# Scan products of two states by transposes on TensorE, 128-row products in the row norm and the last layer

## Chip, core and metric

The kernel runs on one core of a Trainium2 chip. The metric is the device time of one execution in microseconds (us). Three runs of the kernel before took 34249.87 to 34259.34 us, with a median of 34252.28. The engines are TensorE (PE, with its weight loads PEld), VectorE (DVE), ScalarE (ACT) and GpSimd (POOL). SyncE (SP) issues the DMAs of this stage. Each engine works through its own queue in the order of the program.

## The reference

Four layers follow each other on an image of 256 x 256 positions with 128 channels, each as x = x + layer(group norm of x). Layer 0 is an attention along rows, with a layer norm ahead of it (the "row norm"). Layer 1 is a selective scan in four directions. Layer 2 is a spectral layer with two small dense layers behind it. Layer 3 (the "last layer") is a gated recurrence of 16 steps with spectra of small kernels. Almost all of the change lies in the scan of layer 1:

```
x_dbl = einsum('bkdl,kcd->bkcl', xs, x_proj_w)
dts, Bs, Cs = split(x_dbl, [8, 8 + 16], axis=2)
delta = softplus(einsum(dts, dt_w) + dt_bias)
dA = exp(delta * A[d, n])
h[n] = dA * h[n] + (delta * x) * B[n]      # n = 0..15, one step for each position
y = sum over n of h[n] * C[n]
```

There are 256 inner channels d (two halves of 128, dh = 0 and 1), 16 states n, 65536 positions, and four directions k (rows, columns, and both backwards).

## The kernel before

The scan is done by `scan_stream`. A chunk is 512 positions of one direction, so there are 4 x 128 = 512 chunks, one after the other. Partitions are the 128 channels of one half, the free axis is positions. A chunk has eight steps s = 0..7, numbered through as g = 8 ch + s. Step s handles the half dh = s % 2 and the four states from 4 (s // 2) on. So steps 6 and 7 hold states 12 to 15. The loop is software-pipelined by hand: all engines run in program order, and the order of the lines in the loop is the order in each queue. The names used from here on:

- **b(j)**, the B product of step j, in the loop's count (b(8) to b(10) are steps 0 to 2 of the next chunk): delta * x times B for four states, 128 x 2048 elements, L763. GpSimd does steps 2, 4 and 6, VectorE the others. `b_order` says at which step a product is issued. The factor delta * x of the first half is in a PSUM bank (`mm`) with a copy in SBUF for GpSimd (L752); that of the second half is in the PSUM bank `du1`.
- **The scans**: each step has two, s6h0 and s6h1 for step 6. One scan, L796, runs over two states at once (1024 elements). Before it ScalarE writes exp(delta * A) for both states into one of two PSUM tiles `das` (L781, two activations), and then puts the carried state into the middle element of the B product (L785). Lists of extra work, `extras`, are issued behind each scan.
- **c(s)**, the C product, 128 x 2048, by GpSimd, L811.
- **sums(s)**: TensorE adds the four states of c(s) into the y bank with an identity matrix, L830, two steps later. Each product of 512 columns in float32 stands in the trace as two instructions.
- **For the next chunk**, in between: dt (L699, TensorE) and softplus on ScalarE (L711, L712, L718, L719) with a sum on TensorE (L725), delta * x on VectorE (L741), xproj (L667, TensorE), which gives B and C of the chunk after it; they go through DRAM.
- **The loads**: B and C come back from DRAM, spread over all partitions, as loads of 1 MB for four states each (L687 for B, L693 for C). A B load serves two products, b(2i) and b(2i + 1). B and C each have three buffers. At the end of the odd steps SP is given one B load and then one C load:

```python
if s % 2 == 1:
    load_b(g // 2 + 4)
    load_c(g // 2 + 3)
```

So the C load of s1 takes the buffer that c(0) and c(1) read. The results y are stored from step 2 of every even chunk (L643), 1 MB for two chunks, on the same queue.

In the row norm (`row_norm`, blocks of 2048 positions), TensorE centers (L141), takes variances (L163), and spreads the reciprocal root of each position over the partitions by a product with one row of ones (L183). In the last layer (64 blocks), products of 14 rows make the spectra (L1447), and VectorE does most of the gated steps; L1463 adds a constant and L1560 takes 1 - t, both on VectorE.

Of the kernel before, what the change touches and what calls it, by code (L numbers as in the profile page):

```python
# [10 lines left out]
F32 = mybir.dt.float32  # L11
# [16 lines left out]
class Ctx:  # L28


    def __init__(self, tc, t, pool):
        self.tc, self.nc, self.t = tc, tc.nc, t
        nc = self.nc
        self.ident = load(nc, pool, t["c_ident"], "ident")
        self.avg128 = load(nc, pool, t["c_avg128"], "avg128")
        self.gavg = load(nc, pool, t["c_gavg"], "gavg")
        self.ones = pool.tile([P, P], F32, name="ones")
        nc.vector.memset(self.ones, 1.0)
        self.eps = pool.tile([P, 1], F32, name="eps")
        nc.vector.memset(self.eps, 1e-5)  # L40

        self.stats = [pool.tile([P, NCH, 6], F32, name=f"stats{i}") for i in range(2)]
        self.pool = pool

# [6 lines left out]

def group_norm_coef(c, stats, name):

    nc = c.nc
    ab = c.pool.tile([P, 2], F32, name=f"ab_{name}")
    with c.tc.tile_pool(name=f"gn_{name}", bufs=1) as sb, c.tc.tile_pool(
        name=f"gnp_{name}", bufs=1, space=PSUM
    ) as ps:
        mv = sb.tile([P, 2], F32, name="gn_mv")
        nc.vector.bn_aggr(mv, stats)  # L60
        mean = ps.tile([P, 1], F32, name="gn_mean")
        nc.tensor.matmul(mean, c.gavg, mv[:, 0:1], start=True, stop=True)
        off = sb.tile([P, 1], F32, name="gn_off")
        nc.vector.tensor_tensor(off, mv[:, 0:1], mean, ALU.subtract)
        part = sb.tile([P, 1], F32, name="gn_part")
        nc.vector.scalar_tensor_tensor(part, off, off, mv[:, 1:2], ALU.mult, ALU.add)
        var = ps.tile([P, 1], F32, name="gn_var")
        nc.tensor.matmul(var, c.gavg, part, start=True, stop=True)
        sd = sb.tile([P, 1], F32, name="gn_sd")
        nc.scalar.activation(sd, var, AF.Sqrt, bias=c.eps)  # L70
        nc.vector.reciprocal(ab[:, 0:1], sd)
        nc.vector.scalar_tensor_tensor(ab[:, 1:2], mean, -1.0, ab[:, 0:1], ALU.mult, ALU.mult)
    return ab


# [26 lines left out]
def row_norm(c, x, zs, bs, ab):  # L102
# [6 lines left out]
    with ExitStack() as a:  # L109
# [14 lines left out]
        shift = one.tile([P, 1], F32, name="l0_shift")  # L124
        nc.vector.tensor_copy(shift, sp)
        scaled = one.tile([P, P], F32, name="l0_scaled")
        nc.vector.tensor_scalar(scaled, cent, ab[:, 0:1], None, ALU.mult)
# [51 lines left out]
        def spread(m):  # L179
            bc = bcs[m] = ps1.tile([P, 2, CH], F32, name="l0a_bc")  # L180
            for j in range(2):
                r = slice(32 * (m % 2 * 2 + j), 32 * (m % 2 * 2 + j) + 1)
                nc.tensor.matmul(bc[:, j], c.ones[r], rss[m // 2][r], start=True, stop=True)  # L183

# [387 lines left out]
def scan_stream(c, xc2, y, w):  # L572
# [5 lines left out]


    tc, nc = c.tc, c.nc  # L580
    G, BL, NG = 4, 1024, 8
    R = y[1].shape[3]
    NW = BL // S
    on_pool = (2, 4, 6)
    b_order = {0: (3,), 1: (4,), 2: (5,), 3: (6, 7), 4: (8,), 6: (10,)}
    chunks = []
# [4 lines left out]
    with ExitStack() as a:  # L591
# [7 lines left out]

        xds = [st.tile([64, CH], F32, name=f"l1b_xd{i}") for i in range(3)]  # L600
        for s in states:
# [5 lines left out]


        mm = ps1.tile([P, CH], F32, name="l1b_mm")
        du1 = ps1.tile([P, CH], F32, name="l1b_du")  # L610
        blocks, bcs, bbs, ccs, soft, dls, dbs, hs, hcs = ({} for _ in range(9))

# [62 lines left out]
        def xd_copy(ch):  # L675
            if ch >= N:
                return
            xd = xds[ch % 3]
            nc.scalar.copy(xd[:40], du1[:40])
            bc = bcs[ch] = dram.tile([32, CH], F32, name="l1b_bc")  # L680
            nc.sync.dma_start(bc, xd[8:40])

        def load_b(m):
            if m < 4 * N:
                n0 = m % 4 * G
                bb = bbs[m] = bcp.tile([P, G, CH], F32, name="l1b_bb")
                nc.sync.dma_start(bb, bcs[m // 4][n0 : n0 + G][None].to_broadcast([P, G, CH]))  # L687

# [7 lines left out]
        def dt(ch, dh):  # L696
            if ch >= N:
# [3 lines left out]
                w["dt"][:, chunks[ch][0], dh * P : dh * P + P],  # L701
                xds[ch % 3][0:41],
                start=True,
# [50 lines left out]
        def b_product(g):  # L754
            ch, j = divmod(g, NG)
            if ch >= N:
                return
            db = dbs[g] = wk.tile([P, G, CH], F32, name="l1b_db", bufs=5)
            if j in on_pool:
                eng, du = nc.gpsimd, dls[ch, "du"]  # L760
            else:
                eng, du = nc.vector, du1 if j % 2 else mm
            eng.tensor_tensor(db, bbs[g // 2], du[:, None, :].to_broadcast([P, G, CH]), ALU.mult)  # L763

        def scans(g, extras):
# [7 lines left out]
            for i in range(2):  # L773
                one, two = n0 + 2 * i + rev, n0 + 2 * i + 1 - rev
                da = das[i].rearrange("p g t -> p (g t)")
                if g == 0 or ch == N // 2 and j == 0:
                    nc.vector.memset(da[:, mid : mid + 1], 0.0)
                for n in (one, two):
                    o = n % 2 * CH
# [3 lines left out]
                    )  # L783
                first = db[:, 2 * i * CH + mid : 2 * i * CH + mid + 1]
                nc.scalar.activation(  # L785
                    first,
                    states[k][:, dh, two : two + 1],
                    AF.Identity,
                    scale=af[:, two : two + 1],
                    bias=first,  # L790
                )
                sl = slice(2 * i * CH, 2 * i * CH + 2 * CH)
                h_, a_, d_ = hf[:, sl], da, db[:, sl]
                if rev:
                    h_, a_, d_ = h_[:, ::-1], a_[:, ::-1], d_[:, ::-1]
                nc.vector.tensor_tensor_scan(  # L796
                    h_, a_, d_, states[k][:, dh, one : one + 1], ALU.mult, ALU.add
                )
                if i == 0 and g:
                    keep_state(g - 1)  # L800
# [49 lines left out]
        for m in range(3):  # L850
            load_b(m)
            load_c(m)
        for dh in range(2):
            dt(0, dh)
# [8 lines left out]
        b_product(2)  # L863
        load_b(3)
        for ch in range(N):
            nxt = ch + 1
            for s in range(NG):
# [7 lines left out]
                for j in b_order.get(s, ()):  # L875
                    b_product(NG * ch + j)
                extras = [[], []]
                if s == 1:
                    extras[1] = [lambda: soft_abs(nxt), lambda: y_out(ch - 1, 0)]
# [6 lines left out]
                if s == 5:  # L886
                    extras = [[lambda: soft_abs(nxt)], [lambda: soft_exp(nxt)]]
                if s == 6:
                    extras[1] = [lambda: xd_copy(ch + 2)]
                if s == 7:  # L890
                    extras[0] = [lambda: delta_x(nxt, 1), lambda: b_product(g + 2)]
                    extras[1] = [lambda: delta_copy(nxt, 1)]
                if s == 0:
                    dt(nxt, 0)
                scans(g, extras)
                if s == 2:
                    soft_sum(nxt)
                if s == 4:
                    dt(nxt, 1)
                if s == 5:  # L900
# [3 lines left out]
                if g >= 2:  # L904
                    sums(g - 2)
                c_product(g)
                if s % 2 == 1:
                    load_b(g // 2 + 4)
                    load_c(g // 2 + 3)
# [208 lines left out]

def layer1(c, x1, x2p, x2, ab, stats):
    tc = c.tc  # L1120
    with ExitStack() as ctx:
# [6 lines left out]
        with tc.tile_pool(name="l1_w", bufs=1) as wp:  # L1128
# [4 lines left out]
            scan_stream(c, (xc, xct), y, w)  # L1133
        scan_end(c, x1, ab, y[2], y[3], x2p, x2, stats)

# [244 lines left out]
def layer3(c, x3, out, spec, ab):  # L1380
# [9 lines left out]
    with ExitStack() as a:  # L1390
# [22 lines left out]
        nc.vector.tensor_scalar(less, c.ident, -1.0, None, ALU.mult)  # L1413
        phase = load(nc, one, t["c_phase_w"], "l3_phase")
        tiny = one.tile([P, 1], F32, name="l3_tiny")
# [19 lines left out]
        def spectra(b):  # L1435
# [3 lines left out]
            nc.sync.dma_start(k["x"], x3[:, bass.ts(b, BL)])  # L1439
            tu = io.tile([14, 4, 256], F32, name="l3_tu", bufs=2)  # L1440
            nc.sync.dma_start(tu, spec[bass.ts(b, 4)].rearrange("u r f -> r u f"))

# [19 lines left out]
            more = tmp.tile(half, F32, name="l3_more")  # L1462
            nc.vector.tensor_scalar(more, mag, 1e-8, None, ALU.add)  # L1463
            k["inv"] = inverse(more, 1.0, "l3_m")
# [49 lines left out]
        def steps(b):  # L1514
# [44 lines left out]
            have["x"] = new("x")  # L1559
            nc.vector.tensor_scalar(w["x"], w["t"], -1.0, 1.0, ALU.mult, ALU.add)  # L1560
            have["den"] = new("den")
# [72 lines left out]
def program(tc, t, out):  # L1634
    with ExitStack() as ctx:
# [7 lines left out]
        spec = dram.tile([S, 14, 256], F32, name="l3_spec")  # L1643
        with ExitStack() as a:
            kernel_spectra(c, spec, a)
            stream_stats(c, t["x"], c.stats[0])
        layer0(c, t["x"], x1, group_norm_coef(c, c.stats[0], "0"), c.stats[1])
        layer1(c, x1, x2p, x2, group_norm_coef(c, c.stats[1], "1"), c.stats[0])
        layer2(c, x2p, x2, x3, group_norm_coef(c, c.stats[0], "2"), c.stats[1])
        layer3(c, x3, out, spec, group_norm_coef(c, c.stats[1], "3"))  # L1650

# [90 lines left out]
```

## Time and profile before

| | us |
|---|---|
| median of three runs | 34252.28 |
| the profiled execution | 34251.71 |
| its span | 34249.9 |
| stretch from 8000 to 24000 us: scans | 5126 |
| VectorE's scans L796 in it, mean of one | 2.336 |
| GpSimd's C products L811 in it, mean of one | 4.528 |
| B products of VectorE L763, mean of one | 2.274 |
| TensorE instruction of a sum L830, mean of one | 0.639 |

The page gives busy time for each engine, then the span in 40 slices with a digit for the busy tenths, and the granted TensorE clock. A group of instructions reads: line, engine, operation, tiles written and read, shape, count, busy time, mean of one, and the idle time of the engine ahead of it with what ended it. On the timeline a row is: start, length, engine, line, operation, tiles, count, and in brackets the wait. Lengths of two instructions on one engine overlap a little at their ends, so the distance from start to start is what counts in a sum.

### The profile page before, as it was taken

How to read it: one execution, taken by the hardware profiler on the slowest of the kernel's cores; microseconds unless marked ns; L12 is line 12 of the kernel's file. 1: busy time of each engine (PE TensorE's matmuls, PEld its weight loads, DVE VectorE, ACT ScalarE, POOL GpSimd, SP SyncE). 2: the span in 40 equal slices, each digit the busy share in tenths (PEclk: the TensorE clock that was granted, in tenths of full speed). 3: DMA queues.
4: the chain of work that ended last, by engine and by line, in shares of the span. 5: the costliest groups of instructions: out<-in, count | busy, mean ns of one | idle time of the engine just before them, and what ended most of it. 6: DMA issues, size and time to landing. Idle time of an engine off the chain costs nothing. (4 is left out here: it accounts for less than half of the span.)

```text
span 34249.9 us, 256893 instructions
## 1 busy us (share of the span) xinstructions
PE 29062.3 (85%) x72308; PEld 12164.1 (36%) x72308; DVE 31137.1 (91%) x23801; ACT 22770.2 (66%) x46991; POOL 27433.4 (80%) x6996
## 2 busy tenths in 40 slices
PE   7999888888888888888888888888888888899988
PEld 3554333333333333333333333333333333334444
DVE  6668999999999999999999999999999999863699
ACT  3667777777777777777777777777777777532476
POOL 2446899999999999999999999999999999620000
PEclk8999999999999999999999999999999999999888
DMA  3113455555555555555555555555555555674111
GB/s 142 45 45 121 183 191 190 192 189 192 191 190 191 190 192 189 192 191 190 197 201 200 201 203 201 201 201 200 200 201 203 201 201 201 212 236 148 63 34 33
DMA packets 2076530, 5947.88 MB, mean 174 GB/s; under 512 B 115207, under 2 KB 1379608, under 8 KB 1499222
## 3 DMA queue, kind: packets, MB, share of 16 engines
q1 hardware_dynamic: 1939122, 5860.18, 47.3%
q10 hardware_dynamic: 135972, 71.27, 0.7%
q8 instruction: 570, 9.34, 0.1%
q14 instruction: 866, 7.09, 0.1%
HBM read 5238.41 MB, written 692.58 MB: 173 GB/s over the span
## 5 line engine op out<-in xcount | busy, mean ns | idle before, releaser
L796 DVE TENSOR_TENSOR_SCAN l1b_h<-l1b_da,l1b_state,l1b_db 128x1024 f32<-128x1024 f32 x8192 | 18792.7, 2336 | 596.9 <-ACT l1b_db L785 583.3
L811 POOL TENSOR_TENSOR l1b_hc<-l1b_h,l1b_cc 128x2048 f32<-128x2048 f32 x4096 | 18447.2, 4528 | 329.0 <-DVE l1b_h L796 328.0
L830 PE MATMUL l1b_y<-l1b_hc,ident 128*128 128x512 f32 x32768 | 16062.5, 639 | 1117.0 <-POOL l1b_hc L811 1117.0
L781 ACT ACTIVATE l1b_da<-l1b_dl,l_alog 128x512 f32<-128x512 f32 (+1 forms) x16384 | 11297.5, 690 | 3156.6 <-DVE l1b_h L796 2848.7
L830 PEld LDWEIGHTS l1b_y<-l1b_hc,ident 128*128 128x128 f32 x32768 | 6528.7, 205 | 10690.6 <-issue 8162.7
L763 POOL TENSOR_TENSOR l1b_db<-l1b_bb,l1b_dus 128x2048 f32<-128x2048 f32 x1536 | 6967.3, 4536 | 44.5 <-DMA l1b_bb<-l1b_bc 44.5
L763 DVE TENSOR_TENSOR l1b_db<-l1b_bb,l1b_du 128x2048 f32<-128x2048 f32 x2048 | 4657.8, 2274 | 35.2
L785 ACT ACTIVATE l1b_db<-l1b_state,l1b_db,l1b_af 128x1 f32<-128x1 f32 x8192 | 3045.2, 372 | 0.0
L699 PE MATMUL l1b_mm<-l1b_xd,l_dtw 41*128 41x512 f32 x2048 | 1373.1, 755 | 1712.6 <-ACT l1b_dus L752 1706.8
L725 PE MATMUL l1b_mm<-l1b_tail,ident 128*128 128x512 f32 x2048 | 1292.2, 717 | 1380.9 <-ACT l1b_tail L719 1378.5
L807 ACT COPY l1b_state<-l1b_h 128x4 f32<-128x4 f32 x4095 | 789.6, 193 | 2433.8 <-DVE l1b_h L796 2433.7
L327 POOL TENSOR_TENSOR l0b_e<-l0b_e,l0b_den 128x1024 f32<-128x1024 f32 x512 | 969.0, 1893 | 1373.4 <-DVE l0b_den L326 727.3
L725 PE MATMUL l1b_mm<-l1b_relu,ident 128*128 128x512 f32 x2048 | 1308.8, 728 | 0.0
L699 PEld LDWEIGHTS l1b_mm<-l1b_xd,l_dtw 41*128 41x128 f32 x2048 | 337.8, 206 | 2526.4 <-ACT l1b_dus L752 2129.9
L752 ACT COPY l1b_dus<-l1b_mm 128x512 f32<-128x512 f32 x512 | 299.6, 585 | 1388.5 <-DVE l1b_db L763 1388.1
L763 DVE TENSOR_TENSOR l1b_db<-l1b_bb,l1b_mm 128x2048 f32<-128x2048 f32 x512 | 1171.5, 2288 | 18.2 <-ACT l1b_dus L752 0.7
L303 DVE CUSTOM_DVE_ANT_0 l0b_e<-l0b_sc,l0b_bias 128x256 f32<-128x256 f32 x2048 | 745.4, 420 | 414.5 <-PE l0b_sc L292 411.1
L725 PEld LDWEIGHTS l1b_mm<-l1b_tail,ident 128*128 128x128 f32 x2048 | 376.8, 206 | 2051.5 <-ACT l1b_tail L719 1803.9
L318 ACT ACTIVATE l0b_e<-l0b_e,l0b_top 128x256 f32<-128x256 f32 x2048 | 1012.1, 498 | 0.9 <-DVE l0b_top L303 0.9
L667 PE MATMUL l1b_du<-l1b_xc,l_xproj 128*40 128x512 f32 x2048 | 979.8, 601 | 32.2 <-DMA l1b_xc<-l_xc 31.4
L733 ACT COPY l1b_dl<-l1b_mm 128x512 f32<-128x512 f32 x1024 | 587.4, 574 | 524.2 <-DVE l1b_du L741 517.1
L981 POOL TENSOR_TENSOR l1c_y<-l1c_y,l1c_yt 128x512 f32<-128x512 f32 x256 | 396.3, 1570 | 593.1 <-DMA l1c_y<-l_y 528.4
(275 smaller groups left out, 30094.6 us busy)
## 6 DMA issues: line engine op xcount, KB each, us to landing
l1b_bb<-l1b_bc SPq DMA_DIRECT2D x2048, 1024.0 KB
l1b_cc<-l1b_bc SPq DMA_DIRECT2D x2048, 1024.0 KB
l1b_xc<-l_xc SPq DMA_DIRECT2D x128, 1024.0 KB
l_y<-l1b_yo SPq DMA_DIRECT2D x128, 1024.0 KB
l1b_xc<-l_xct SPq DMA_DIRECT2D x256, 512.0 KB
l_y<-l1b_yo SPq DMA_DIRECT2D x256, 512.0 KB
l_xc<-l1a_o SPq DMA_DIRECT2D x64, 1024.0 KB
l_xct<-l1a_ot SPq DMA_DIRECT2D x16, 4096.0 KB
```

The costliest lines, as they stand in the source:

```text
L318: nc.scalar.activation(e[:, i], e[:, i], AF.Exp, scale=-1.0, bias=top[:, i : i + 1], accum_out=den[:, i : i + 1],)
L327: nc.gpsimd.tensor_tensor(e, e, den[:, :, None].to_broadcast([P, 4, S]), ALU.mult)
L667: nc.tensor.matmul(du1[:40], w["xproj"][:, dh, k, :], in_block(blocks[ch][0], ch, dh), start=dh == 0, stop=dh == 1,)
L699: nc.tensor.matmul(mm, w["dt"][:, chunks[ch][0], dh * P : dh * P + P], xds[ch % 3][0:41], start=True, stop=True,)
L725: nc.tensor.matmul(mm, c.ident, part, start=i == 0, stop=i == 1)
L763: eng.tensor_tensor(db, bbs[g // 2], du[:, None, :].to_broadcast([P, G, CH]), ALU.mult)
L781: nc.scalar.activation(da[:, o + lo : o + hi], dl[:, lo:hi], AF.Exp, scale=w["A"][:, k, dh, n : n + 1])
L785: nc.scalar.activation(first, states[k][:, dh, two : two + 1], AF.Identity, scale=af[:, two : two + 1], bias=first,)
L796: nc.vector.tensor_tensor_scan(h_, a_, d_, states[k][:, dh, one : one + 1], ALU.mult, ALU.add)
L807: nc.scalar.copy(states[k][:, dh, n0 : n0 + G], hs[g][:, :, 0 if k >= 2 else CH - 1])
L811: nc.gpsimd.tensor_tensor(hc, hs[g], ccs[g // 2], ALU.mult)
L830: nc.tensor.matmul(ys[j % 2], c.ident, hc[:, i], start=False, stop=j // 2 * G + i == 15)
```

## The change

In the scan, the products with B of states 14 and 15 are no longer made by b(6) and b(7), which now cover two states (T = 14). They are made with positions on the partitions: TensorE transposes delta * x of both halves (`du_turn`) and the B rows (`b_turn`). ScalarE copies them out (`du_keep`, `b_keep`, `du1_copy`) and makes the product of two states and four blocks of 128 positions as eight activations with a scale for each partition (`b_scale`). TensorE turns the result back, eight transposes for each half (`turn_back`), into the PSUM tile `das[1]`, which is then the scan's input; the exp of these two scans, s6h1 and s7h1, goes to an SBUF tile. B keeps two buffers instead of three, the products four and two small ones instead of five, the projections two instead of three. The B loads are issued at other steps. Elsewhere, the spread of the row norm uses a selector with 128 rows, the 14 rows of the last layer are padded with zeros to 128, two of its operations go from VectorE to ScalarE, and the statistics live in pools of their own.

```diff
-    b_order = {0: (3,), 1: (4,), 2: (5,), 3: (6, 7), 4: (8,), 6: (10,)}
+    T, NT = 14, CH // P
+    b_order = {0: (3,), 1: (4,), 2: (5,), 3: (6, 7), 4: (8,)}
+    turned_at = {(0, 1): (0, 1), (1, 0): (2,), (2, 0): (3,), (3, 0): (4,), (4, 1): (5, 6, 7)}
...
         def load_b(m):
             if m < 4 * N:
-                n0 = m % 4 * G
-                bb = bbs[m] = bcp.tile([P, G, CH], F32, name="l1b_bb")
-                nc.sync.dma_start(bb, bcs[m // 4][n0 : n0 + G][None].to_broadcast([P, G, CH]))
+                n0, n = m % 4 * G, min(G, T - m % 4 * G)
+                bb = bbs[m] = bcp.tile([P, G, CH], F32, name="l1b_bb", bufs=2)
+                nc.sync.dma_start(
+                    bb[:, 0:n], bcs[m // 4][n0 : n0 + n][None].to_broadcast([P, n, CH])
+                )
...
+        def b_turn(ch):
+            for b in range(NT):
+                nc.tensor.transpose(
+                    du1[:, bass.ts(b, 40)], xds[ch % 2][0:40, bass.ts(b, P)], c.ident[0:40, 0:40]
+                )
...
+        def du_turn(ch, dh):
+            du = dls.pop((ch, "du1")) if dh else dls[ch, "du"]
+            for b in range(NT):
+                nc.tensor.transpose(mm[:, bass.ts(b, P)], du[:, bass.ts(b, P)], c.ident)
+
+        def du_keep(ch, dh):
+            nc.scalar.copy(duts[ch][:, :, dh], mm.rearrange("p (b c) -> p b c", b=NT))
+
+        def b_scale(ch, i):
+            n, b = divmod(i, NT)
+            nc.scalar.activation(
+                turned[ch][:, b, n], duts[ch][:, b], AF.Identity, scale=bts[ch][:, b, n : n + 1]
+            )
+
+        def turn_back(ch, dh, to):
+            for n in range(16 - T):
+                for b in range(NT):
+                    nc.tensor.transpose(to[:, n, bass.ts(b, P)], turned[ch][:, b, n, dh], c.ident)
...
+                    nc.scalar.activation(
+                        from_state, states[k][:, dh, last : last + 1], AF.Identity,
+                        scale=af[:, last : last + 1],
+                    )
+                    turn_back(ch, dh, das[i])
+                    dbp, da = da, das_t.rearrange("p g t -> p (g t)")
...
+                if s == 0:
+                    extras[0] = [lambda: du_keep(ch, 1)]
...
+                if s == 5:
+                    extras[0].insert(0, lambda: b_keep(nxt))
...
-                    extras[0] = [lambda: delta_x(nxt, 1), lambda: b_product(g + 2)]
-                    extras[1] = [lambda: delta_copy(nxt, 1)]
+                    extras[0] = [
+                        lambda: delta_x(nxt, 1),
+                        lambda: b_product(g + 2),
+                        lambda: b_product(g + 3),
+                    ]
+                    extras[1] = [
+                        lambda: delta_copy(nxt, 1),
+                        lambda: du1_copy(nxt),
+                        lambda: du_turn(nxt, 0),
+                    ]
+                scans(g, extras)
                 if s == 0:
                     dt(nxt, 0)
-                scans(g, extras)
+                if s == 7:
+                    du_keep(nxt, 0)
...
                 if s == 4:
+                    b_turn(nxt)
                     dt(nxt, 1)
...
                 if g >= 2:
                     sums(g - 2)
+                if s == 7:
+                    du_turn(nxt, 1)
                 c_product(g)
+                if s in (0, 2, 3, 7):
+                    load_b(4 * ch + {0: 3, 2: 4, 3: 5, 7: 6}[s])
                 if s % 2 == 1:
-                    load_b(g // 2 + 4)
                     load_c(g // 2 + 3)
...
-                r = slice(32 * (m % 2 * 2 + j), 32 * (m % 2 * 2 + j) + 1)
-                nc.tensor.matmul(bc[:, j], c.ones[r], rss[m // 2][r], start=True, stop=True)
+                nc.tensor.matmul(
+                    bc[:, j], pick[:, m % 2 * 2 + j], rss[m // 2], start=True, stop=True
+                )
...
-        phase = load(nc, one, t["c_phase_w"], "l3_phase")
+        phase = one.tile([P, S], F32, name="l3_phase")
+        nc.vector.memset(phase, 0.0)
+        nc.sync.dma_start(phase[0:14], t["c_phase_w"])
...
-            nc.vector.tensor_scalar(more, mag, 1e-8, None, ALU.add)
+            nc.scalar.activation(more, mag, AF.Identity, bias=tiny)
...
-            nc.vector.tensor_scalar(w["x"], w["t"], -1.0, 1.0, ALU.mult, ALU.add)
+            nc.scalar.activation(w["x"], w["t"], AF.Identity, scale=-1.0, bias=c.ones[:, 0:1])
```

## The prediction

> **What bounds the kernel now.** I read the busy times and slices first, then the groups, then one chunk of the scan loop on the timeline, engine by engine, and last the waits of the DMA queue.
>
> ```profile
> PE 29062.3 (85%) x72308; PEld 12164.1 (36%) x72308; DVE 31137.1 (91%) x23801; ACT 22770.2 (66%) x46991; POOL 27433.4 (80%) x6996
> ...
> POOL 2446899999999999999999999999999999620000
> PEclk8999999999999999999999999999999999999888
> ```
>
> Slices 5 to 34 are one steady stage, the scan loop: 512 chunks, about 25.6 of 34.2 ms. What is worth anything is decided there. In a stretch of 16000 us inside it there are 5126 scans, 16 to a chunk, so a chunk takes 49.94 us.
>
> VectorE and GpSimd are both at 97 to 99% there. Which of them leads is seen on the timeline of one chunk (VectorE, then GpSimd, then the DMA queue of SP):
>
> ```profile
> 16012.39 9.07 DVE L796 TENSOR_TENSOR_SCAN l1b_h<-l1b_da,l1b_state,l1b_db 128x1024 f32<-128x1024 f32 x4
> 16021.38 2.26 DVE L763 TENSOR_TENSOR l1b_db<-l1b_bb,l1b_du 128x2048 f32<-128x2048 f32 x1
> 16028.18 2.29 DVE L763 TENSOR_TENSOR l1b_db<-l1b_bb,l1b_du 128x2048 f32<-128x2048 f32 x1
> 16035.59 2.29 DVE L763 TENSOR_TENSOR l1b_db<-l1b_bb,l1b_mm 128x2048 f32<-128x2048 f32 x1
> 16045.37 2.35 DVE L796 TENSOR_TENSOR_SCAN l1b_h<-l1b_da,l1b_state,l1b_db 128x1024 f32<-128x1024 f32 x1 [0.62 <-ACT l1b_db L785]
> ...
> 16017.21 4.51 POOL L811 TENSOR_TENSOR l1b_hc<-l1b_h,l1b_cc 128x2048 f32<-128x2048 f32 x1 [0.67 <-DVE l1b_h L796]
> 16021.69 4.53 POOL L763 TENSOR_TENSOR l1b_db<-l1b_bb,l1b_dus 128x2048 f32<-128x2048 f32 x1
> 16026.18 8.99 POOL L811 TENSOR_TENSOR l1b_hc<-l1b_h,l1b_cc 128x2048 f32<-128x2048 f32 x2
> ...
> 16030.73 0.32 SPq L693 DMA_DIRECT2D l1b_cc<-l1b_bc  x1
> 16031.14 1.28 SPq L643 DMA_DIRECT2D l_y<-l1b_yo  x2
> 16032.52 4.16 SPq L687 DMA_DIRECT2D l1b_bb<-l1b_bc  x1
> ```
>
> The reader is to see three things. GpSimd waits 0.67 us for VectorE once a chunk, at C-product 0 (s0, after its second scan, at 16016.9). So VectorE leads and GpSimd is carried along with little to spare. From there GpSimd does c(0), b(4), c(1) without a gap, and c(1) ends 13.8 us after that scan, at 16030.68. At that moment, and not earlier, SP issues the C load of s1, then the y store of an even chunk, then the B load behind them: the queue had stood at the C load, as its own waits say:
>
> ```profile
> SPq L693 <- POOL l1b_hc L811: 12106.3, 1282, 17.2
> ```
>
> (This answer is for the stretch from 8000 to 24000 us.) That B load, of s3 in the kernel before, is not needed before s7. How long it takes is in the table of busy time by stretch, whose lines end with granted clock, DMA share and GB/s:
>
> ```profile
> 16084.00:16086.00 2.00, 0.40 (x1) 0.00 (x0) 1.97 (x3) 0.62 (x3) 2.00 (x2) 1.00 1.01 406
> 16086.00:16088.00 2.00, 0.00 (x0) 0.00 (x0) 2.00 (x2) 0.14 (x1) 2.00 (x1) 1.00 0.50 209
> 16039.00:16042.00 3.00, 3.00 (x4) 0.88 (x4) 2.98 (x2) 2.78 (x6) 3.00 (x2) 0.50 0.80 333
> 16042.00:16045.00 3.00, 3.00 (x5) 1.04 (x4) 2.75 (x2) 2.43 (x6) 3.00 (x2) 0.51 0.00 0
> ```
>
> In the next chunk (odd, no store) c(1) ended at 16080.6, and the engines ran at 406 GB/s until about 16087. In the even one they ran until 16041.4. I took the landing of this B load from the DMA records of all chunks 8 to 503: a median of 7.15 us after the end of c(1) in odd chunks, and 11.5 to 11.8 in even chunks of the first two directions (the last two have a y load ahead as well, which the new order puts behind).
>
> [...] SP stood 12106 us in that stretch at the C loads. [...] after the 3 to 4 us idle before L699 it shows 0.50 above. [...]
>
> **The change, part by part.** Times are counted in one chunk; s6h1 is the second scan of step 6.
>
> *Removed.* b(7) on VectorE works on 1024 instead of 2048 elements: a product follows another after 2.2 us (16035.59 to 16037.80), so -1.1. b(6) on GpSimd halves too, -2.3, which only lengthens its wait at c(0). A memset of one column costs VectorE 0.1 (59 ns by L777).
>
> *ScalarE* gets eight copies of 128x256 (0.38 us in L1478 to 0.5 in L318, where a scale or bias is read from memory), three of 128x512 at 0.58 (L752), and small ones: 5.6 to 6.6 us beside 35.2 of 49.9 now. In s0 to s3 they fit into waits it has. The three after s4 delay s5 and s6: up to 0.4, hidden by the next item; if that cover goes, they cost the 0.4.
>
> *TensorE* gets 28 transposes of 0.116 us (eight of L336 start within 0.93), 3.2 us beside 41.8 of 49.9. Eight of them stand in s6 before s6h1, in the queue behind: dt (L699), sums(2), xproj, sums(3). dt starts 0.76 us after b(8) ends (16087.74 to 16088.50), because the copy L752 waits for b(8). From dt to the end of sums(3) the trace has 12.35 us in the mean of 320 chunks (10.06 to 13.4; 22 instructions at the full-clock spacing of 0.43 would be 9.5, the rest is the halved clock). Then 1.1 for the transposes, 0.45 for the activation on their result: s6h1 can start 14.7 us after b(8), where it starts 12.7 after it now (16087.74 to 16100.4). So +2.0. The wait before dt gets longer below, so the clock stays halved; 0 and +3.0 are the ends. The other eight (s7) have 1.2 us of room behind a VectorE product, and the copies around s0h1 0.8, worked out in the same way; I take 0 and keep 0.5 for the top of the range.
>
> *The B loads, moved.* With two buffers instead of three, the load for b(8) goes from s1 to the end of s2. Before, it was issued ahead of the C load of s1 (16067.03, for a b(8) at 16085.5). Now it stands behind that C load and, in even chunks, behind the y store: the position of the old s3 load shown above. So it lands 13.8 + 7.2 = 21.0 us after the second scan of s0 in odd chunks and 13.8 + 11.6 = 25.4 in even ones. VectorE wants to start b(8) at 20.9 - 2.2 - 1.1 = 17.6 (20.9 is the distance from that scan's end to b(8)'s end now). With 0.1 for the semaphore b(8) is late by 3.5 and 7.9 us, in the mean 5.7. Behind b(8) on VectorE stand all scans of s4, and behind these everything else, so nothing hides it. The other moved loads have room: that for b(7) lands some 6 us after that scan and is wanted at 11.3; that for b(9) is a chunk half early.
>
> *Moved without a price.* b(10) goes on GpSimd from before c(6) to behind it; it is wanted in s2 of the next chunk, and c(6) comes 4.5 us earlier for it. dt for the next chunk's first half goes behind the scans of s0 and waits for a ScalarE copy there; behind it on TensorE stand sums(6), whose result is read in s1, one step later. The third buffer of the projections and the fifth of the products are given up; their readers are a chunk old when they are written again.
>
> Sum for a chunk: -1.1 + 0.1 + 2.0 + 5.7 = +6.7, of which the second scan of s0 to b(8) is 25.5 and the rest 31.15, 56.65 in all. Times 512: +3430 us.
>
> *Row norm.* The spread with 128 rows does not run two at a time: four take 2.0 us by the 0.43 spacing, not 1.13, but four L141 at halved clock take 3.78 and at full clock 1.98. One of each is on the loop of 13.65 us a block: -1.1, times 32 = -35 (ends -80, +45).
>
> *Last layer.* VectorE bounds it (193 of 200 us). Two operations of 420 ns leave it, 0.84 times 64 blocks = -54; its wait of 1.1 us for L1454, behind 14-row products at halved clock, should halve: -32. Together -85 (-30 to -125). Buffers made elsewhere cost nothing visible.
>
> Total: the profiled execution took 34251.7 us, 0.6 under the median of the runs; 34251.7 + 3430 - 120 = 37560.
>
> **Rivals.**
> A. Loads late, but TensorE in time: 5.7 - 1.0 = 4.7 a chunk, 36540. For it: chunks of 10.06 us exist. Against: the idle time before dt grows.
> B. Only TensorE late: the loads are in time, +1.0 a chunk, 34640. It needs SP not to stand at c(1).
> C. Stores do not hold up the load, all chunks like odd ones: 3.5 - 1.0 + 2.0 = 4.5, 36440.
> D. Faster: GpSimd, with 2.3 us less to do, gets ahead and frees the queue early. VectorE's 1.0 then counts: -510 - 120, 33620. Its place is c(1); it decides if c(1) ends within 10.3 us of the scan in odd chunks and 5.9 in even ones. Against: three operations of 4.5 us follow that scan in order, and GpSimd already waits for it.
>
> **How the numbers follow.** Likeliest 0.70; A 0.10, C 0.06, B 0.04, D 0.10. The likeliest's own range: lateness 5.3 to 6.0, TensorE 0 to 3.5, so 4.4 to 8.6 a chunk: with the other stages 36.3 to 38.7 ms. It holds A and C too, 0.86 less the tails; I take 36200 to 38700. Faster by over 0.2% is D, 0.09; within 0.2%, which is about what can be told from no change, 0.01; slower 0.90.
>
> **What would show it.** In the groups of after: L763's DVE product waiting for DMA l1b_bb, some 5 us a chunk, about 2.9 ms in all, more in even chunks; a scan of s6 waiting for ScalarE behind a PE transpose, about 2 us; VectorE near 84% in the stage; GpSimd idle. If the product shows no wait for the DMA, the main step is wrong. If the scan stage is right but the end is off by 100 us, the row norm and last layer are.

## The result and the profile after

The changed kernel takes 37966.18 us (median of four runs, 37961.58 to 37974.88), the kernel before, run beside it, 34254.60 (four runs). The ratio is 1.1083, with a 95% interval of 1.1070 to 1.1097. The forecast was 37560, within 36200 to 38700.

The profiled execution took 37974.88 us, with a span of 37973.0. Its page (busy time, then two rows of the 40 slices):

```profile
PE 30758.7 (81%) x86644; PEld 13723.6 (36%) x86644; DVE 30793.3 (81%) x24192; ACT 25197.1 (66%) x54287; POOL 26438.6 (70%) x6996
...
DVE  6669888888888888888888888888888888884499
...
POOL 2447788888888888888888888888888888840000
```

No engine is full any more in the scan stage: VectorE's slices fell to 8, GpSimd's from 9 to 8. By its table of busy time from 8000 to 24000 us, VectorE works 13418.59 of these 16000 us (84%), where it worked 15592.81 before. So the loop waits for something that is not an engine. The page's chain, followed back from the last instruction, names it; so do two of the groups (busy time and mean, then the idle time ahead and who ended it):

```profile
DVE 36%; PE 25%; DMA 12%; POOL 9%; issue 5%; ACT 5%; SPq 0%; DVEq 0%; POOLq 0%; ACTq 0%
...
L782 DVE TENSOR_TENSOR l1b_db<-l1b_bb,l1b_mm 128x2048 f32<-128x2048 f32 x512 | 1171.5, 2288 | 2856.2 <-DMA l1b_bb<-l1b_bc 2856.2
L882 DVE TENSOR_TENSOR_SCAN l1b_h<-l1b_dat,l1b_state,l1b_da 128x1024 f32<-128x1024 f32 x1024 | 2400.3, 2344 | 1065.9 <-ACT l1b_da L878 1065.9
```

The first group is b(8), once in each of the 512 chunks; it stands still for 2856.2 us in all, 5.58 a chunk, and always for its B load. The second holds s6h1 and s7h1, 1065.9 us. On the timeline of two chunks, an odd one and then an even one (VectorE, GpSimd, SP's queue; the wait is in brackets):

```profile
16038.88 2.29 DVE L782 TENSOR_TENSOR l1b_db<-l1b_bb,l1b_mm 128x2048 f32<-128x2048 f32 x1 [3.11 <-DMA l1b_bb<-l1b_bc]
...
16055.90 2.35 DVE L882 TENSOR_TENSOR_SCAN l1b_h<-l1b_dat,l1b_state,l1b_da 128x1024 f32<-128x1024 f32 x1 [1.70 <-ACT l1b_da L878]
...
16098.42 2.29 DVE L782 TENSOR_TENSOR l1b_db<-l1b_bb,l1b_mm 128x2048 f32<-128x2048 f32 x1 [8.19 <-DMA l1b_bb<-l1b_bc]
...
16116.39 2.35 DVE L882 TENSOR_TENSOR_SCAN l1b_h<-l1b_dat,l1b_state,l1b_da 128x1024 f32<-128x1024 f32 x1 [2.64 <-ACT l1b_da L878]
...
16027.30 9.03 POOL L901 TENSOR_TENSOR l1b_hc<-l1b_h,l1b_cc 128x2048 f32<-128x2048 f32 x2
...
16031.88 0.32 SPq L710 DMA_DIRECT2D l1b_cc<-l1b_bc  x1
16032.30 6.67 SPq L702 DMA_DIRECT2D l1b_bb<-l1b_bc  x2
...
16086.34 0.32 SPq L710 DMA_DIRECT2D l1b_cc<-l1b_bc  x1
16086.75 1.53 SPq L658 DMA_DIRECT2D l_y<-l1b_yo  x2
16088.45 4.99 SPq L702 DMA_DIRECT2D l1b_bb<-l1b_bc  x2
```

The GpSimd row holds c(1) and c(2) of 4.5 us each, so c(1) ends at 16031.8. At 16031.88 SP gets past the C load of s1 and at 16032.30 issues the B load (the first of the two in that row). b(8) can start 6.6 us after that, and VectorE has been idle for 3.11 us. In the even chunk the y store stands between C load and B load, and the idle time is 8.19.

For all that follows, chunks are compared by the distances between VectorE's starts, as means over chunks 8 to 503 (even and odd ones each half). "To b(8)" runs from the start of the first scan of s1, which stands right behind the second scan of s0, to the start of b(8); the other columns run from scan start to scan start (s4h0 is the first scan of s4, s5h1 the second of s5). All in us, from the traces:

| kernel | to b(8), even / odd | s4h0 to s5h0 | s5h0 to s5h1 | s6h0 to s6h1 | s7h1 to s0h0 | chunk |
|---|---|---|---|---|---|---|
| before | 18.70 / 18.70 | 4.63 | 2.94 | 2.27 | 4.45 | 49.95 |
| after | 25.55 / 21.13 | 5.24 | 2.67 | 4.45 | 4.67 | 57.36 |

The difference of 7.41 a chunk is 4.64 at b(8), 2.18 at s6h1, 0.34 in s4 and s5 together, 0.22 at s0h0 and 0.03 elsewhere. By stages, the time from the first scan to the end of the last one goes from 25570.0 to 29346.9 us, which is +3777; the row norm takes about 12 us less and the last layer about 42.

### The profile page after: what moved, and what is told of

Read it like the earlier page. It is cut to its first block, busy times and chain, and to the rows that moved or that the text cites. A ratio compares the mean times of both kernels' runs of the same rounds, so it can differ in the third digit from the quotient of the medians.

```text
span 37973.0 us, 292667 instructions
## 1 busy us (share of the span) xinstructions
PE 30758.7 (81%) x86644; PEld 13723.6 (36%) x86644; DVE 30793.3 (81%) x24192; ACT 25197.1 (66%) x54287; POOL 26438.6 (70%) x6996
## 4 chain that ended last, share of the span: by engine, by line
DVE 36%; PE 25%; DMA 12%; POOL 9%; issue 5%; ACT 5%; SPq 0%; DVEq 0%; POOLq 0%; ACTq 0%
DVE l1b_h L882 21%; PE l1b_y L920 13%; DMA l1b_bb<-l1b_bc 11%; DVE l1b_db L782 7%; POOL l1b_hc L901 6%; POOL l1b_db L782 3%; PE l1b_mm L716 3%; PE l1b_du L682 2%; DVE l1a_mm L526 1%; PE l2f_fp L1453 1%; PE l1b_da L836 1%; PE l2f_op L1460 1%; ACT l1b_da L868 1%; DVE l1b_dbs L782 1%; DVE l1b_du L758 1%
## 5 line engine op out<-in xcount | busy, mean ns | idle before, releaser
L882 DVE TENSOR_TENSOR_SCAN l1b_h<-l1b_da,l1b_state,l1b_db 128x1024 f32<-128x1024 f32 x6144 | 14203.2, 2340 | 472.8 <-ACT l1b_state L897 262.4
L868 ACT ACTIVATE l1b_da<-l1b_dl,l_alog 128x512 f32<-128x512 f32 (+1 forms) x14336 | 9881.3, 689 | 682.1 <-DVE l1b_h L882 438.8
L716 PE MATMUL l1b_mm<-l1b_xd,l_dtw 41*128 41x512 f32 x2048 | 1635.5, 889 | 3941.1 <-ACT l1b_dus L769 3586.6
L782 POOL TENSOR_TENSOR l1b_db<-l1b_bb,l1b_dus 128x2048 f32<-128x2048 f32 x1024 | 4694.3, 4584 | 43.7 <-DMA l1b_bb<-l1b_bc 43.7
L782 DVE TENSOR_TENSOR l1b_db<-l1b_bb,l1b_du 128x2048 f32<-128x2048 f32 x1536 | 3513.8, 2288 | 39.2 <-ACT l1b_db L874 2.4
L782 DVE TENSOR_TENSOR l1b_db<-l1b_bb,l1b_mm 128x2048 f32<-128x2048 f32 x512 | 1171.5, 2288 | 2856.2 <-DMA l1b_bb<-l1b_bc 2856.2
L882 DVE TENSOR_TENSOR_SCAN l1b_h<-l1b_dat,l1b_state,l1b_da 128x1024 f32<-128x1024 f32 x1024 | 2400.3, 2344 | 1065.9 <-ACT l1b_da L878 1065.9
L882 DVE TENSOR_TENSOR_SCAN l1b_h<-l1b_da,l1b_state,l1b_dbs 128x1024 f32<-128x1024 f32 x1024 | 2393.5, 2337 | 263.2 <-ACT l1b_dbs L874 261.1
L874 ACT ACTIVATE l1b_db<-l1b_state,l1b_db,l1b_af 128x1 f32<-128x1 f32 x6144 | 2283.9, 372 | 0.0
L716 PEld LDWEIGHTS l1b_mm<-l1b_xd,l_dtw 41*128 41x128 f32 x2048 | 405.2, 246 | 4124.6 <-ACT l1b_dus L769 3646.6
L829 ACT ACTIVATE l1b_dbt<-l1b_dut,l1b_bt 128x256 f32<-128x256 f32 x4096 | 1886.0, 496 | 0.0
L868 ACT ACTIVATE l1b_dat<-l1b_dl,l_alog 128x512 f32<-128x512 f32 (+1 forms) x2048 | 1349.8, 706 | 0.0
L782 POOL TENSOR_TENSOR l1b_dbs<-l1b_bb,l1b_dus 128x1024 f32<-128x1024 f32 x512 | 1207.5, 2358 | 0.0
```

The lines of the kernel that those rows point to most:

```text
L716: nc.tensor.matmul(mm, w["dt"][:, chunks[ch][0], dh * P : dh * P + P], xds[ch % 2][0:41], start=True, stop=True,)
L782: eng.tensor_tensor(db, bbs[g // 2][:, 0:n], du[:, None, :].to_broadcast([P, n, CH]), ALU.mult)
L829: nc.scalar.activation(turned[ch][:, b, n], duts[ch][:, b], AF.Identity, scale=bts[ch][:, b, n : n + 1])
L868: nc.scalar.activation(da[:, o + lo : o + hi], dl[:, lo:hi], AF.Exp, scale=w["A"][:, k, dh, n : n + 1])
L874: nc.scalar.activation(first, state, AF.Identity, scale=af[:, two : two + 1], bias=first)
L882: nc.vector.tensor_tensor_scan(h_, a_, d_, states[k][:, dh, one : one + 1], ALU.mult, ALU.add)
```

## The experiments

Theory: a B load that SP reaches only after c(1) makes b(8) late, and TensorE, which waits for that, then works at half clock (0.50 from 16041.8 to 16045.2 us, in the odd chunk above), which makes s6h1 late. Rivals: two B buffers instead of three are too few wherever the load stands; the y store is what holds the load up; TensorE's added work makes s6h1 late by itself. A third B buffer in the changed kernel was not tried; the second experiment below answers it with the kernel before.

**The C load behind the B load (e1_c_behind_b, and the same kernel again as e1_timed).**

```diff
-                if s % 2 == 1:
+                if s == 2:
+                    load_c(4 * ch + 3)
+                if s in (3, 5, 7):
                     load_c(g // 2 + 3)
```

> Theory (queue position: the B load for b(8) stands behind the C load of s1, which waits for c(1)): the wait of b(8) for the DMA, 5.57 us a chunk in the changed kernel, goes to under 0.3, a chunk takes 51.8 us instead of 57.36, the whole about 35.1 ms (34.9 to 35.3). Rival 1 (the third B buffer is what is missing, or the DMA engines are too slow for 1 MB): the wait stays at 3 us or more, over 36.5 ms. Rival 2 (TensorE's late transposes set the chunk, and the DMA wait is only where the slack shows): the DMA wait goes and another of the same size takes its place, over 37.5 ms.

It took 34208.1 us in one run, beside 34246.02 for the kernel before. That is less than the 34.9 to 35.3 ms expected, which still had TensorE late at s6h1. The same kernel in more runs:

> The kernel with the C load of s1 behind the B load of s2 again, timed against the kernel before. Theory: the scans are level with the kernel before (49.98 against 49.95 us a chunk) and the other stages give 54 us, so a ratio of 0.9985 to 0.9995. Rival: the single look was off, and it is level or slower.

34225.07 us (12 runs), ratio to before 0.9993, interval 0.9984 to 1.0001: no difference that can be told. The timeline of one chunk of the first run (VectorE, then TensorE, then SP's queue):

```profile
16026.53 2.29 DVE L782 TENSOR_TENSOR l1b_db<-l1b_bb,l1b_mm 128x2048 f32<-128x2048 f32 x1
...
16041.77 2.32 DVE L882 TENSOR_TENSOR_SCAN l1b_h<-l1b_dat,l1b_state,l1b_da 128x1024 f32<-128x1024 f32 x1
...
16028.96 0.44 PE L791 MATMUL l1b_du<-ident,l1b_xd 40*128 40x40 f32 x4
16029.49 1.12 PE L716 MATMUL l1b_mm<-l1b_xd,l_dtw 41*128 41x512 f32 x2
...
16039.55 1.04 PE L836 MATMUL l1b_da<-ident,l1b_dbt 128*128 128x128 f32 x8
...
16018.67 0.53 SPq L702 DMA_DIRECT2D l1b_bb<-l1b_bc  x1
16022.63 0.33 SPq L710 DMA_DIRECT2D l1b_cc<-l1b_bc  x1
```

The B load goes out 4 us ahead of the C load, and b(8) has no bracket, so it doesn't wait. s6h1 has none either, although the transposes L836 stand ahead of it as they did: dt (L716) follows the turn of B without a gap, and the transposes start 10.06 us after dt, at a granted clock of 1.00 all the way, instead of 12.7 (16041.84 to 16054.50) in the odd chunk above and 13.6 in the even one. The distances are 17.78 to b(8) and 2.65 to s6h1 (some of these scans still wait), the chunk 49.98. So one place in a queue makes 7.38 of the 7.41 us: 23.34 - 17.78 = 5.56 directly and 4.45 - 2.65 = 1.80 through s6h1. Two B buffers are enough. What remains of the change in the scan is worth nothing: b(8) comes 0.92 earlier by the shorter b(7), and s4 to s5 (+0.34), s6h1 (+0.38) and s0h0 (+0.22) take it back.

**The kernel before, with the loads at the new places (e4_before_b_late).** It keeps three B buffers and has no transposes.

```diff
-        load_b(3)
         for ch in range(N):
...
+                if s in (0, 2, 3, 7):
+                    load_b(4 * ch + {0: 3, 2: 4, 3: 5, 7: 6}[s])
                 if s % 2 == 1:
-                    load_b(g // 2 + 4)
                     load_c(g // 2 + 3)
```

> The kernel before, with its three B buffers and none of the transposes, but with the B loads issued at the steps of the change. Theory: b(8) wants to start 18.7 us after the second scan of s0 here, and its load lands at 21.1 (odd) and 25.5 (even) as in the changed kernel, so it waits 2.4 and 6.9 us, 4.6 in the mean; a chunk takes 54.6 us, the whole 36.6 ms (36.3 to 36.9). Rival (the wait comes from two buffers or from the turned products): within 0.1 ms of the kernel before.

36573.82 us, as expected. Its timeline (VectorE in an even and an odd chunk, SP in the odd one):

```profile
16035.03 2.29 DVE L763 TENSOR_TENSOR l1b_db<-l1b_bb,l1b_mm 128x2048 f32<-128x2048 f32 x1 [6.61 <-DMA l1b_bb<-l1b_bc]
16087.26 2.29 DVE L763 TENSOR_TENSOR l1b_db<-l1b_bb,l1b_mm 128x2048 f32<-128x2048 f32 x1 [2.33 <-DMA l1b_bb<-l1b_bc]
...
16080.11 0.32 SPq L693 DMA_DIRECT2D l1b_cc<-l1b_bc  x1
16080.53 0.85 SPq L687 DMA_DIRECT2D l1b_bb<-l1b_bc  x2
```

The third buffer doesn't help here: the B load goes out 0.42 us after the C load, as it does with two buffers (16031.88 and 16032.30 in the odd chunk above). To b(8) are 25.51 and 20.99, within 0.14 of the changed kernel, every other distance is as before, and the chunk is 54.50, that is 4.55 more, all of it at b(8).

**The y store behind the B load (e2_store_behind).**

```diff
-            if dh == 1 and ch % 2 == 1:
-                block_dma(y[k], k, i, yo, True)
+            if dh == 1 and ch == N - 1:
+                y_store(ch)
...
+                if s == 2:
+                    y_store(ch - 1)
```

> Theory (the y store of even chunks ahead of the B load makes the difference between 8.2 and 3.1 us of waiting): even chunks fall to about 55 us as the odd ones, the mean chunk to 55.1, the whole to 36.8 ms (36.6 to 37.0). Rival (even chunks are late for another reason, the store only being there too): even chunks stay near 59.7 us, the whole at 37.97 ms.

37321.29 us, a miss in size: some 650 less than after, where about twice as much had been expected. The timeline of an even chunk (VectorE, SP):

```profile
16058.60 2.29 DVE L782 TENSOR_TENSOR l1b_db<-l1b_bb,l1b_mm 128x2048 f32<-128x2048 f32 x1 [4.65 <-DMA l1b_bb<-l1b_bc]
...
16050.09 0.32 SPq L710 DMA_DIRECT2D l1b_cc<-l1b_bc  x1
16050.58 0.32 SPq L702 DMA_DIRECT2D l1b_bb<-l1b_bc  x1
16050.99 2.26 SPq L658 DMA_DIRECT2D l_y<-l1b_yo  x2
```

The load goes out first, and yet b(8) starts 8.0 us after its issue, where 6.6 were enough in the odd chunk above. To b(8) are now 22.67 in even chunks: the store ahead of the load cost 4.42 us, and behind it still 1.53. Even without any store, b(8) would be late by the 21.1 of odd chunks against 17.78. So the store makes the wait longer; it is not the cause.

**TensorE filled while it waits (e5b_filled).** Products that nobody reads stand ahead of dt, 12 or 18 of them:

```diff
                     b_turn(nxt)
+                    if ch + 1 < N:
+                        for i in range(12 if ch % 2 else 18):
+                            nc.tensor.matmul(
+                                du1[:, 256:512], c.ident, dls[ch, 1][:, 0:256], start=True, stop=True
+                            )
                     dt(nxt, 1)
```

> The changed kernel with 12 (odd chunks) and 18 (even) products of 128x256 that nobody reads, put on TensorE into its idle time ahead of dt. Theory (after the idle time dt, sums(2) and xproj run at half clock, and this makes s6h1 late): from dt to the transposes takes about 10 us instead of 12.7 to 13.6, the scan s6h1 waits under 0.4 us instead of 2.1, a chunk takes 55.3 us, the whole 36.9 ms (36.7 to 37.2). Rival (the length of the queue at full clock makes it late, or more work only adds): the wait at s6h1 stays at 2 us or grows, 37.9 ms or more.

37263.3 us, a little over the expected range; the chunk is 55.93, which is 1.43 less. First TensorE's timeline after, in an odd chunk, then that of the filled kernel, in an even one:

```profile
16041.84 2.07 PE L716 MATMUL l1b_mm<-l1b_xd,l_dtw 41*128 41x512 f32 x2 [5.86 <-ACT l1b_dus L769]
16043.83 5.36 PE L920 MATMUL l1b_y<-l1b_hc,ident 128*128 128x512 f32 x8
16049.12 1.91 PE L682 MATMUL l1b_du<-l1b_xc,l_xproj 128*40 128x512 f32 x4
16050.96 3.70 PE L920 MATMUL l1b_y<-l1b_hc,ident 128*128 128x512 f32 x8
```

```profile
16020.27 8.04 PE L1017 MATMUL l1b_du<-l1b_dl,ident 128*128 128x256 f32 x36
16029.62 1.12 PE L716 MATMUL l1b_mm<-l1b_xd,l_dtw 41*128 41x512 f32 x2 [1.31 <-ACT l1b_dus L769]
16030.67 3.70 PE L920 MATMUL l1b_y<-l1b_hc,ident 128*128 128x512 f32 x8
```

In the trace after, dt, sums(2), xproj and sums(3) follow each other in this order in all 278 whole chunks from 8000 to 24000 us. The same two instructions of dt take 2.07 us after 5.86 of idle time, and 1.12 after the fill; the eight behind them 5.36 and 3.70. The table by stretch gives the granted clock (the last three columns are clock, DMA share, GB/s), first after, then filled:

```profile
16038.40:16041.80 3.40, 0.00 (x0) 0.00 (x0) 2.92 (x2) 0.60 (x2) 3.40 (x2) 0.79 0.61 239
16041.80:16045.20 3.40, 3.36 (x4) 1.33 (x5) 3.38 (x2) 3.35 (x7) 1.29 (x1) 0.50 0.53 169
16045.20:16048.60 3.40, 3.40 (x7) 1.25 (x5) 2.88 (x2) 3.35 (x9) 2.58 (x1) 0.71 1.00 348
```

```profile
16029.60:16033.00 3.40, 3.38 (x8) 1.43 (x9) 3.38 (x2) 3.33 (x8) 0.00 (x0) 1.00 0.23 96
```

From s6h0 to s6h1 odd chunks now take 2.65 us as in the first experiment, and even ones 3.08. So TensorE isn't late by its added work, or by little of it: it is late by working at half clock (0.50) after the wait for the load. The saving is 0.6 short of what was expected: b(8) starts 0.17 later than after in the mean, and the even chunks keep part of theirs; from 8000 to 24000 us dt still waits in 152 of 286 chunks. The granted clock is 0.50 right behind 5.86 us of idle time, and 1.00 behind 1.31; what idle time it takes was not measured.

**dt behind the sums (e5_dt_behind_sums).**

```diff
                 if s == 4:
                     b_turn(nxt)
-                    dt(nxt, 1)
...
                 if g >= 2:
                     sums(g - 2)
+                if s == 4:
+                    dt(nxt, 1)
```

> The changed kernel with its late load, and on TensorE in s4 the sums(2) ahead of dt instead of behind it. Theory (s6h1 is late because 22 instructions at half clock stand between the copy that waits for b(8) and the transposes): sums(2) goes into the idle time, 8 of the 22 leave that stretch, the wait at s6h1 falls from 2.1 us to under 0.3, and s6h0 to s6h1 from 4.4 to 2.3 us; the wait of b(8) for the DMA stays at 5.6. A chunk takes 55.2 us, the whole 36.85 ms (36.7 to 37.1). Rival (the transposes wait for ScalarE's products or for the PSUM tile, not for the queue): s6h0 to s6h1 stays over 4 us, the whole at 37.9 ms.

37466.52 us, half met: from s6h0 to s6h1 are 3.40 us instead of 4.45, not the 2.3 that were expected. TensorE's timeline, odd chunk:

```profile
16055.42 1.12 PE L716 MATMUL l1b_mm<-l1b_xd,l_dtw 41*128 41x512 f32 x2
16059.59 1.91 PE L682 MATMUL l1b_du<-l1b_xc,l_xproj 128*40 128x512 f32 x4 [3.05 <-ACT l1b_bt L799]
```

In this chunk dt doesn't wait and takes 1.12 us (in the even one before it, 2.07 behind a wait of 5.71), but xproj right behind it writes where the turned B stands, and waits 3.05 us for ScalarE's copy of it (L799): one wait has moved to the next instruction of the queue.

**Row norm and last layer without the scan's part (e7_padded_only).** The kernel before, with the selector of 128 rows and the padded spectra alone; the two operations of the last layer stay on VectorE.

```diff
-                nc.tensor.matmul(bc[:, j], c.ones[r], rss[m // 2][r], start=True, stop=True)
+                nc.tensor.matmul(
+                    bc[:, j], pick[:, m % 2 * 2 + j], rss[m // 2], start=True, stop=True
+                )
...
-            tu = io.tile([14, 4, 256], F32, name="l3_tu", bufs=2)
-            nc.sync.dma_start(tu, spec[bass.ts(b, 4)].rearrange("u r f -> r u f"))
+            tu = tus[b % 2]
+            nc.sync.dma_start(tu[0:14], spec[bass.ts(b, 4)].rearrange("u r f -> r u f"))
```

> The kernel before with the two paddings to 128 rows alone (row norm and spectra of the last layer); the two operations of the last layer stay on VectorE, the scans are as before. In the changed kernel the row norm went from 446.0 to 434.3 us and the last layer from 2145.8 to 2103.5. Theory: the row norm gains the same 12; of the last layer's 42 the padding has the smaller part, about 10 to 20, since VectorE bounds it and 0.84 us a block leave VectorE only with the moved operations; the whole is 25 us (20 to 35) under the kernel before. Rival (the last layer gained by the clock alone): 42 in the last layer, 54 in all. Second rival (padding gains nothing there): 12 in all.

34221.86 us in one run, 31.5 under the median of the kernel before on that chip, whose 15 runs lie within 11 us. By stages the row norm takes about 12 less and the last layer about 20 less (17 to 22, by the engine whose first and last instructions are taken). VectorE's wait for the spectra, over 1200 us of the last layer, first here, then in the changed kernel:

```profile
DVE l_sq L1465 <- ACT l_amp L1463: 30.7, 37, 1.2
```

```profile
DVE l_sq L1584 <- ACT l_amp L1582: 41.1, 37, 1.4
```

Over as long a stretch of the kernel before it is 40.3 us in 36 waits. Padding shortens the wait from 1.12 to 0.83 a block; moving two operations off VectorE lets it arrive earlier and wait 1.11 again.

**Three orders at once (e8_three_orders).** The edits of the first experiment and of dt behind the sums, and three of ScalarE's scaled copies of s4 put ahead of its copy of delta * x:

```diff
-    turned_at = {(0, 1): (0, 1), (1, 0): (2,), (2, 0): (3,), (3, 0): (4,), (4, 1): (5, 6, 7)}
+    turned_at = {(0, 1): (0, 1), (1, 0): (2,), (2, 0): (3,), (3, 0): (4,)}
...
-                    extras[0] = [lambda: du_copy(nxt)]
+                    extras[0] = [lambda i=i: b_scale(ch, i) for i in (5, 6, 7)]
+                    extras[0].append(lambda: du_copy(nxt))
```

> The changed kernel with three orders altered: the C load of s1 behind the B load of s2, sums(2) ahead of dt in s4, and the three turned products of s4 ahead of the copy that waits for b(8), where ScalarE stands for 2.7 us. Theory: with the C load alone a chunk takes 49.98 us; the wait of s6h1 for TensorE (0.35) and the longer waits of s5 and s6 for ScalarE (0.33) go, and a chunk takes 49.3 us, the whole 33.85 ms (33.7 to 34.0), 1.2% under the kernel before. Rival (GpSimd, at 95% of that stage, or another ScalarE wait takes it back): 34.1 to 34.2 ms as with the C load alone.

33968.2 us (four runs, 33961.76 to 33972.55), ratio to before 0.9917, interval 0.9902 to 0.9932: 0.8% under the kernel before, with the whole interval under 1, and within the range expected. The chunk is 49.51, where 49.3 had been expected. VectorE's timeline has s6h1 without a wait; the first line is s5h1, where most of what s5h0 gained has turned up as a wait for ScalarE:

```profile
16022.72 2.35 DVE L882 TENSOR_TENSOR_SCAN l1b_h<-l1b_da,l1b_state,l1b_db 128x1024 f32<-128x1024 f32 x1 [1.06 <-ACT l1b_db L874]
...
16027.85 2.32 DVE L882 TENSOR_TENSOR_SCAN l1b_h<-l1b_dat,l1b_state,l1b_da 128x1024 f32<-128x1024 f32 x1
```

Against the first experiment s4h0 to s5h0 went from 5.24 to 4.63, s5h0 to s5h1 from 2.67 to 3.15, and s6h0 to s6h1 from 2.65 to 2.32. The first two lie at the moved copies and gain 0.13 together, the third lies at dt and gains 0.33; the sum of 0.46 is the 0.47 of the chunk, times 512 = 241 us. The copies and dt were not run apart in this order of the loads.

## Why the prediction was right, and where its terms were off

The range held rivals A and C as well, so the total alone doesn't tell them from the likeliest; the distances at each place do.

**The load (+5.7 forecast, 5.56 measured).** The step that carried the forecast held as stated: c(1) frees SP's queue, the B load lands 7.2 or 11.6 us later, and b(8) starts 21.0 to 25.5 us after the second scan of s0 (measured 21.13 and 25.55). The experiment with the kernel before shows the place in the queue as the cause, with buffers and transposes excluded. It could be priced from the kernel before because that had a load of the same size at that very place, behind the same C load and store, with its landing in the records.

**b(7) (-1.1 forecast, -0.92 measured).** The first experiment shows it without the late load: 17.78 against 18.70. From s1h1 to s3h0, where b(7) stands, the loop is 1.04 shorter (11.24 to 10.20), nearly as forecast. But 0.13 are lost ahead of it: from s1h0 to s1h1 are 2.37 instead of 2.24, since s1h1 now just waits for ScalarE.

**TensorE (+2.0 forecast, 2.18 measured at s6h1).** The forecast had the half clock from dt to sums(3) (in the kernel before 0.50 from 16039 to 16042 us, with dt at 16038.55 behind 3.06 us of idle time), and that it would stay because the wait gets longer; that was the author's estimate, and after the change it is 0.50 behind 5.86 us. The size is near, but the step treated two things as independent that aren't. The rival "only TensorE late" gave 34640 with the loads in time; that kernel takes 34225. With b(8) 0.92 earlier and more to do ahead of dt, TensorE waits there only 1.2 us in the mean of 320 chunks, where it waited 3.3 in the kernel before (us in all, times, longest; first before, then the first experiment, both from 8000 to 24000 us):

```profile
PE l1b_mm L699 <- ACT l1b_dus L752: 1068.9, 320, 4.1
```

```profile
PE l1b_mm L716 <- ACT l1b_dus L769: 396.0, 292, 2.8
```

And TensorE is faster in most chunks: from dt to the transposes it takes under 10.5 us in 231 of these 320, and in none of 279 in the changed kernel; the mean granted clock from 8000 to 24000 us is 0.95 (e1_timed) against 0.89. So 1.80 of the 2.18 belong to the load, and the load's full price is 7.4 a chunk. The rival "TensorE in time, loads late" is excluded by the same link, unless TensorE is given something to do, as the filled kernel shows.

**ScalarE (0 forecast, 0.34 measured in s4 and s5).** Its copies of s0 to s3 were to fit into waits that it has, and the 0.13 at s1h1 above show that they don't quite, though the added work is less than forecast (ScalarE is busy 35.2 us a chunk before and 39.8 in the first experiment, 4.6 more instead of 5.6 to 6.6). For the three after s4, the text gave up to 0.4 if the cover went, and the cover went: the copies delay s5's first scan by 0.61, and only 0.27 comes back. The memset's term (0.1) measured 0.22 at s0h0, with the other things that stand there. Together 0.34 and 0.12 from these two, 0.18 at TensorE and 0.18 at b(7), less 0.14 at the load, are the 0.7 a chunk by which the forecast was short, 3430 against 3777 in the stage.

**Rivals C and D.** Stores that don't hold the load up: refuted, they cost 4.42 in even chunks. GpSimd freeing the queue early: its c(1) still ends 13 to 14 us after the second scan of s0, as it did. Even with the load in time the gain of about 1.0 on VectorE, which that rival counted on, was used up by ScalarE and TensorE.

**Row norm (-35 forecast, -12) and last layer (-85 forecast, -42).** In the row norm the clock term was too large: the center products did speed up, 860 to 752 ns in the mean (granted clock 0.75 to 0.89 from 200 to 500 us), but TensorE still waits 2.3 us a block ahead of them (2.9 before), and VectorE's wait for the spread shrank only from 5.7 to 5.3 us a block (126.4 us in 22 waits, 121.8 in 23), which is 14 us in 32 blocks. In the last layer the padding's term was -32, and with the padding alone the stage fell by about 20. For the two moved operations 54 was forecast, and about 22 remain of it. VectorE's shorter work ran into the wait for the spectra again: 64 blocks times 0.28 is 18 of the missing 32. The cause of the other 14 stays open.

## What to carry to other kernels

When a load changes its place in an issuing queue, ask what the instruction ahead of it waits for and when that ends; look for a load that already stands there and read its landing from the records. Price a late arrival together with what idles meanwhile: here a quarter of its cost came 17 us later, through TensorE's work at half clock (0.50) behind its wait. When work leaves the leading engine, look at each later wait for which it now arrives earlier: in the last layer 18 of 54 us went there, and in the last experiment 0.48 of the 0.61 at s5.

## What the runs showed of the hardware

- **With products padded to 128 rows the granted clock was higher.** In the last layer, where the products of the spectra were padded from 14 rows (e7_padded_only), it went from 0.81 to 0.88 over 1200 us, although TensorE was busy for less time (first before, then padded; the clock is the third number from the end):

```profile
32600.00:33800.00 1200.00, 1016.12 (x2627) 535.40 (x2627) 1159.41 (x1599) 850.77 (x1564) 0.00 (x0) 0.81 0.11 34
```

```profile
32600.00:33800.00 1200.00, 968.16 (x2622) 506.70 (x2622) 1168.90 (x1612) 858.42 (x1569) 0.00 (x0) 0.88 0.11 34
```

  In 300 us of the row norm, with 128 rows instead of 1 in the spread, it rose from 0.75 to 0.89; there TensorE was also busier (249.41 us against 235.89). How the clock depends on the rows was not measured further.
- **With a store right behind it on the queue, the load's product was still late:** with the 1 MB y store issued 0.41 us after the 1 MB B load (16050.99 and 16050.58, e2_store_behind), b(8) started 8.0 us after the load's issue instead of 6.6, and in the mean 1.53 us later than in odd chunks.
- **The wait at the head of SP's queue cost time while the DMA engines had room.** In the changed scan the DMA engines' mean share is 0.43 of the time from 8000 to 24000 us (0.53 before), SP stands 11102.5 us of these at the C loads, and 12% of the kernel's chain is DMA, because the load goes out only when c(1) has ended. With the two loads turned round it is 0%, and b(8) waits for its load 0.8 us in all from 8000 to 24000 us (e1_timed).
